# Expert layers: the gate's weights of a batch in 128 zero-padded rows

## The chip, the cores and the metric

The kernel runs on one core of one Trainium2 chip. The metric is the device time of one execution in microseconds (us). A core has a matrix engine (PE, with its weight loads listed apart as PEld), a vector engine (DVE), a scalar engine (ACT), a general engine (POOL), a queue for transfers (SP), and DMA engines. SBUF is its working memory of 128 rows (partitions); PSUM receives the results of PE in banks of 128 rows x 512 values.

## The reference

The whole model is a "macaron" stack: a mixture-of-experts layer (half weight), linear attention, the same expert layer again, six layers of windowed attention with a feed-forward part, a full attention, and the six layers once more. The change touches only the expert layer, which occurs twice:

```python
probs = jax.nn.sigmoid(x_flat @ Wg + bg)
mask = (probs > THRESHOLD).astype(x_flat.dtype)
weights = probs * mask
h = jax.nn.relu(jnp.einsum('td,edh->eth', x_flat, W1) + b1[:, None, :])
expert_out = jnp.einsum('eth,ehd->etd', h, W2) + b2[:, None, :]
combined = jnp.einsum('te,etd->td', weights, expert_out)
```

There are 8 experts, 128 channels, 512 hidden values, and 2048 tokens in 4 batches of 512. Every expert is computed for every token; its output is multiplied by the token's weight for it and summed.

## The kernel before

**Order.** The program has four parts that follow each other: part 0 (the two expert layers and the linear attention between them, class `Front`), part 1 (six layers), part 2 (full attention), part 3 (six layers). Parts 1 and 3 are issued in an order written out by hand, and so is PE's in part 2. In part 0 a scheduler chooses the order of instructions on each engine from a simulated timeline. Storage comes from pools: each tile has a tag, a tag has a fixed number of buffers, and a new tile of a tag waits until the buffer's old tile has been read for the last time. For PSUM the tag mm has four banks, which hold nearly every product in the kernel.

**The expert layer.** `moe` runs 32 steps, expert outside and batch inside. A step does this:

- `hidden` (L274 to L276, then L931 to L937): for each of four blocks of 128 hidden values PE makes hp from three products of 512 columns (values and weights are kept as a high and a low piece; three of the four products of pieces are used). ACT applies bias and relu (L931, tile r), DVE rounds r to the high piece (L935, tile h), and the low piece is the difference (L937), on POOL for the even blocks and on DVE for the odd ones.
- `output` of the step before (L941 to L957): PE spreads the gate's weights of one expert over 128 rows (L945, tile wbp), ACT copies them out of PSUM (L947, wbs), PE accumulates twelve products of 512 columns (L951 to L953, tile o), DVE multiplies o by wbs (L955, tmp), and POOL adds that to acc (L957; DVE for the last expert).
- At the first batch of an expert, `experts` loads its W1 and W2 by DMA (L874, L875) and splits them on ACT and DVE (L811, L812).
- For expert 0 alone, `gates`: logits (tile lg), sigmoid and threshold on DVE and ACT, the weights as high and low piece (wpieces), transposed to rows by PE (L915), copied to wT by ACT (L917), and the part of the bias b2 (L919, L920).

**How the weights lie.** wT is one tile of 128 rows x 512 tokens. Batch b uses its rows 32b to 32b+15: eight experts' high pieces, then eight low pieces. The other rows are never written. The constant `sel` holds, for each expert, a 128 x 128 matrix with ones in rows 32b+e and 32b+8+e for all four b, so that L945, with the 16 rows of one batch on both sides, gives in each of the 128 output rows the weight of expert e for every token. PE's products around it contract 128 rows.

**Where tiles come from.** wT takes the one buffer of tag ge, whose next user is the feed-forward part of part 1 (L630). `begin` makes wT and acc; it runs at the start of each expert layer. Tag E has two buffers of 4096 bytes a row; in part 1 the softmax writes it (L440).

Of the kernel before, what the change touches and what calls it, by code (L numbers as in the profile page):

```python
# [6 lines left out]
F32 = mybir.dt.float32  # L7
FR = mybir.dt.float32r
# [62 lines left out]
def bank(g, tag, shape=(128, 512), name=None):  # L71
    n = math.prod(shape[1:])
    t = g.psum.tile([128, 1024 if tag == "S" else 512], F32, tag=tag, name=name or tag, bufs=BANKS[tag])[0:shape[0], 0:n]
    if len(shape) > 2:
        d = "abcd"[:len(shape) - 1]
        t = t.rearrange("p (%s) -> p %s" % (" ".join(d), " ".join(d)), **dict(zip(d[1:], shape[2:])))
    return t
# [195 lines left out]
def mm3(nc, out, wh, wl, xh, xl):  # L273
    nc.tensor.matmul(out, lhsT=wh, rhs=xh, start=True, stop=False)  # L274
    nc.tensor.matmul(out, lhsT=wh, rhs=xl, start=False, stop=False)  # L275
    nc.tensor.matmul(out, lhsT=wl, rhs=xh, start=False, stop=True)  # L276
# [543 lines left out]
class Front:  # L820
# [71 lines left out]
    def gates(self, b):  # L892

        nc, g = self.nc, self.g
        t = self.xT[b]
        lg = bank(g, "n2", [128, 4, 8], "lg")
        for k in range(4):
            ks = slice(k * 128, (k + 1) * 128)
            mm3(nc, lg[:, k, :], t[:, 0, ks], t[:, 1, ks], self.wg[:, 0, :], self.wg[:, 1, :])
        z = self.tile("z", [128, 4, 8])  # L900
        e = self.tile("e", [128, 4, 8])
        nc.vector.tensor_tensor(z, lg, self.bg.unsqueeze(1).to_broadcast([128, 4, 8]), ALU.add)
        nc.scalar.activation(e, z, AF.Exp, scale=-1.0)
        nc.vector.tensor_scalar(e, e, 1.0, None, ALU.add)
        nc.vector.reciprocal(e, e)
        nc.vector.scalar_tensor_tensor(e, z, 0.0, e, ALU.is_gt, ALU.mult)
        wp = self.tile("wpieces", [128, 4, 2, 8])
        hi = self.tile("whi", [128, 4, 8], FR)
        nc.scalar.copy(hi, e)
        nc.vector.tensor_copy(wp[:, :, 0, :], hi.bitcast(F32))  # L910
        nc.vector.tensor_tensor(wp[:, :, 1, :], e, hi.bitcast(F32), ALU.subtract)
        p = self.bank("wTp")
        rows = slice(32 * b, 32 * b + 16)
        for k in range(4):
            nc.tensor.matmul(p[rows, k * 128:(k + 1) * 128], lhsT=wp[:, k].rearrange("p a c -> p (a c)"), rhs=g.ident,  # L915
                             start=True, stop=True)
        nc.scalar.copy(self.wT[rows], p[rows])  # L917
        p = self.bank("b2p")
        nc.tensor.matmul(p, lhsT=self.b2[rows], rhs=self.wT[rows].bitcast(F32), start=True, stop=True)  # L919
        nc.scalar.copy(self.acc[:, b, :], p)  # L920

    def hidden(self, ex, b):
# [18 lines left out]
    def output(self, ex, b, hs, w2):  # L941
        nc = self.nc
        wb = self.bank("wbp")
        rows = slice(32 * b, 32 * b + 16)
        nc.tensor.matmul(wb, lhsT=self.sel[rows, ex, :], rhs=self.wT[rows], start=True, stop=True)  # L945
        wbs = self.tile("pt", [128, 512], name="wbs")
        nc.scalar.copy(wbs, wb)  # L947
        o = bank(self.g, ("n2", "av")[b % 2], [128, 512], "o")
        for k in range(4):
            h = hs[k]  # L950
            nc.tensor.matmul(o, lhsT=w2[:, 0, k, :], rhs=h[:, 0, :], start=(k == 0), stop=False)  # L951
            nc.tensor.matmul(o, lhsT=w2[:, 1, k, :], rhs=h[:, 0, :], start=False, stop=False)
            nc.tensor.matmul(o, lhsT=w2[:, 0, k, :], rhs=h[:, 1, :], start=False, stop=(k == 3))  # L953
        tmp = self.tile("t2", [128, 512], name="tmp")
        nc.vector.tensor_tensor(tmp, o, wbs, ALU.mult)  # L955
        a = self.acc[:, b, :]
        (nc.vector if ex == 7 else nc.gpsimd).tensor_tensor(a, a, tmp, ALU.add)  # L957
# [7 lines left out]

    def begin(self):
        self.xT = {}
        self.wT = self.tile("ge", [128, 512], FR, "wT")
        self.acc = self.tile("v", [128, 4, 512], name="acc")
        self.experts(0)  # L970

# [387 lines left out]
```

## Time and profile before

| what | value |
|---|---|
| runs | 4488.29, 4487.82, 4475.41 us; median 4487.82 |
| profiled execution | 4486.91 us, of it 4485.1 us from first to last instruction |
| mean granted clock of PE | 0.939 |
| first and second expert layer | about 12 to 270 us and 325 to 580 us |
| linear attention between them | about 270 to 320 us |
| one expert (four steps) in steady running | 27.55 us |
| six layers, full attention, six layers | from about 580, 2250 and 2780 us |

The profile is one execution. "Busy" is the time in which an engine had an instruction under way; PE's instructions overlap, so that the distance between their starts tells more of its pace than their length. A wait names the instruction that ended last before the waiting one started. The chain of waits is followed back from the end of the program, at each step to what released it.

### The profile page before, as it was taken

The numbers are of one execution on the slowest core, as the hardware profiler recorded it, in microseconds if no ns is written. First come the engines' busy times: TensorE is split into PE (matmuls) and PEld (weight loads), VectorE is DVE, ScalarE is ACT, GpSimd is POOL, SyncE is SP. The second block draws the span as 40 slices with busy tenths as digits, with TensorE's granted clock in tenths as the row PEclk, the third lists the DMA queues.
The fourth block names the chain that finished last, engine by engine and source line by source line (L and its number), as shares of the span: only waits on it lengthen the run. The fifth ranks groups of instructions, "written<-read, shape, count | busy, mean of one in ns | idle before, by whom it ended". The sixth has DMA issues, their size and how long they took to land.

```text
span 4485.1 us, 150251 instructions
## 1 busy us (share of the span) xinstructions
PE 3865.4 (86%) x66435; PEld 2663.9 (59%) x66436; DVE 3705.2 (83%) x6415; ACT 2604.5 (58%) x5050; POOL 2493.1 (56%) x2164
## 2 busy tenths in 40 slices
PE   8989978898888888988869998888889889888886
PEld 5666646666666666666533434566666666566665
DVE  6968978888898888888867776888888888888886
ACT  5434455665565565665536666555656656556563
POOL 4625656666666666666501112666666666666663
PEclk9999989999999999999979999999999999999998
DMA  2000033433434334343331222333343343433432
GB/s 61 19 10 15 22 86 74 90 70 81 88 66 91 71 76 88 70 88 73 84 95 49 69 76 52 70 80 82 72 86 73 78 90 61 89 69 77 85 62 49
DMA packets 163852, 312.44 MB, mean 70 GB/s; under 512 B 41304, under 2 KB 125664, under 8 KB 138176
## 3 DMA queue, kind: packets, MB, share of 16 engines
q0 software_dynamic: 31008, 202.40, 22.8%
q1 hardware_dynamic: 132192, 100.44, 7.8%
q8 instruction: 520, 8.52, 0.8%
q14 instruction: 132, 1.08, 0.1%
HBM read 77.49 MB, written 17.69 MB: 21 GB/s over the span
## 4 chain that ended last, share of the span: by engine, by line
DVE 38%; PE 37%; DMA 12%; issue 6%; ACT 4%; POOL 2%; SPq 1%; ACTq 0%; POOLq 0%; DVEq 0%
DMA xs<-x 10%; DVE sm L448 4%; PE vps L401 3%; DVE h L935 3%; DVE E L440 3%; PE S L428 3%; DVE mx L438 3%; DVE xT L269 3%; PE av L471 3%; DVE rtq L308 3%; PE S L1147 2%; DVE pt L455 2%; PE av L1184 2%; PE qkps L274 2%; PE ST L1176 2%
## 5 line engine op out<-in xcount | busy, mean ns | idle before, releaser
L310 POOL TENSOR_TENSOR raw<-raw,rot 128x512 f32<-128x512 f32 x768 | 1006.8, 1362 | 544.2 <-ACT raw L300 540.4
L300 ACT COPY raw<-qkps 128x512 f32<-128x512 f32 x768 | 453.3, 590 | 662.2 <-PE qkps L276 643.7
L401 PE MATMUL vps<-vo,xF 128*32 128x256 f32 x12288 | 751.6, 386 | 40.0 <-issue 29.3
L401 PEld LDWEIGHTS vps<-vo,xF 128*32 128x32 f32 x12288 | 405.9, 111 | 330.3 <-issue 81.6
L452 POOL TENSOR_TENSOR E<-E,smr 128x1024 f32<-128x1024 f32 x192 | 389.6, 2029 | 310.1 <-DVE smr L450 177.0
L407 ACT COPY vx<-vps 128x512 f32<-128x512 f32 x768 | 427.1, 584 | 108.6 <-PE vps L401 106.7
L303 ACT ACTIVATE sq<-qkps 128x512 f32<-128x512 f32 x768 | 473.1, 616 | 0.0
L443 POOL TENSOR_TENSOR E<-E,rq 128x1024 f32<-128x1024 f32 x192 | 388.8, 2025 | 95.6 <-DVE E L440 57.3
L471 PE MATMUL av<-vx,pt 128*32 128x128 f32 x11904 | 381.6, 275 | 58.1 <-DVE x L478 32.8
L274 PE MATMUL qkps<-xT,wqk 128*128 128x512 f32 x768 | 343.4, 447 | 73.3 <-DVE rtq L308 40.6
L471 PEld LDWEIGHTS av<-vx,pt 128*32 128x32 f32 x11904 | 335.7, 110 | 115.8 <-DVE x L478 49.3
L1148 DVE TENSOR_REDUCE nm<-S 128x1 f32<-128x512 f32 x512 | 325.2, 684 | 63.3 <-PE S L1147 62.7
L308 DVE TENSOR_TENSOR rtq<-qkps,rot 128x512 f32<-128x512 f32 x384 | 259.9, 684 | 134.2 <-ACT sq L303 132.6
L383 DVE TENSOR_TENSOR rtk<-rtk,R 128x512 f32<-128x512 f32 x384 | 254.0, 672 | 104.7 <-PE R L380 104.3
L677 PE MATMUL fout<-w,ge 128*128 128x128 f32 (+1 forms) x1152 | 231.9, 379 | 123.3 <-DVE rtk L383 120.4
L1177 ACT ACTIVATE E<-ST 128x512 f32<-128x512 f32 x512 | 273.8, 599 | 109.3 <-PE ST L1176 109.1
L937 POOL TENSOR_TENSOR h<-r,h 128x512 fp32r<-128x512 f32 x128 | 182.3, 1424 | 251.5 <-DVE h L935 237.9
L275 PE MATMUL qkps<-xT,wqk 128*128 128x512 f32 x768 | 310.9, 405 | 5.7 <-issue 2.9
L276 PE MATMUL qkps<-xT,wqk 128*128 128x512 f32 x768 | 309.4, 403 | 5.0 <-issue 5.0
L428 PE MATMUL S<-rtk,rtq 64*32 64x64 f32 (+1 forms) x24576 | 291.4, 229 | 15.5 <-issue 13.3
L428 PEld LDWEIGHTS S<-rtk,rtq 64*32 64x32 f32 x24576 | 284.1, 108 | 31.3 <-issue 18.1
L677 PEld LDWEIGHTS fout<-w,ge 128*128 128x128 f32 (+1 forms) x1152 | 218.4, 289 | 133.7 <-DVE rtk L383 129.4
(257 smaller groups left out, 8803.8 us busy)
## 6 DMA issues: line engine op xcount, KB each, us to landing
rtk<-raw POOLq DMA_DIRECT2D x192, 512.0 KB, 6.7
rtq<-raw POOLq DMA_DIRECT2D x192, 512.0 KB, 6.5
pd<-pc SPq DMA_DIRECT2D x36, 384.0 KB
wqkr<-in_L_ffn_Wqk SPq DMA_DIRECT2D x192, 64.0 KB
rot<-in_c_rot SPq DMA_DIRECT2D x24, 512.0 KB
k<-pd SPq DMA_DIRECT2D x32, 288.0 KB
r<-in_L_ffn_W SPq DMA_DIRECT2D x32, 256.0 KB
wvraw<-in_L_ffn_WvT SPq DMA_DIRECT2D x24, 256.0 KB
```

The costliest lines, as they stand in the source:

```text
L274: nc.tensor.matmul(out, lhsT=wh, rhs=xh, start=True, stop=False)
L300: nc.scalar.copy(raw, ps)
L303: nc.scalar.activation(sq, ps, AF.Square)
L308: nc.vector.tensor_tensor(self.rt[s][:, i, :], ps, rot[:, 0, :], ALU.mult)
L310: nc.gpsimd.tensor_tensor(raw, raw, rot[:, 1, :], ALU.mult)
L401: nc.tensor.matmul(ps[p * 32:(p + 1) * 32, ww, :], lhsT=xF[:, t0:t0 + 32], rhs=g.vo[(self.l, self.hf, p // 2)][:, p % 2, :], start=True, s ...
L407: nc.scalar.copy(self.v[th][:, 2 * t:2 * t + 2, :], ps)
L428: nc.tensor.matmul(self.S[k][p * 32:(p + 1) * 32, ab, w * 64 + 64 - n:w * 64 + 64], lhsT=self.rt[1][rows, p, t0:t0 + 32], rhs=self.rt[0][r ...
L443: nc.gpsimd.tensor_tensor(E4, E4, self.rq[:, :, 8 * k:8 * k + 8].unsqueeze(3).to_broadcast([128, 2, 8, 64]), ALU.mult)
L452: nc.gpsimd.tensor_tensor(E, E, r.unsqueeze(2).to_broadcast([128, 16, 64]), ALU.mult)
L471: g.nc.tensor.matmul(self.av[ww * 32:(ww + 1) * 32, k, :], lhsT=self.pt[w // 8][:, ab, w % 8, role, :], rhs=self.v[src // 8][:, src % 8, a ...
L677: nc.tensor.matmul(self.o[:, t, :], lhsT=h[0:k, t * 128:(t + 1) * 128], rhs=g.F[self.l].w2[0:k, i, :], start=(i == 0 and t == 0), stop=(i ...
```

## The change

wT becomes four arrays of 128 rows x 512 tokens, one for each batch, two to a tile of tag E. Both tiles are filled with zeros on POOL in `begin`. Batch b's 16 rows are written where they were before, at 32b, in its own array. The spreading product takes all 128 rows of `sel` and of the batch's array; the rows of other batches are zero there. The bias product (L919) keeps its 16 rows.

```diff
-        nc.scalar.copy(self.wT[rows], p[rows])
+        nc.scalar.copy(self.wT[b][rows], p[rows])
         p = self.bank("b2p")
-        nc.tensor.matmul(p, lhsT=self.b2[rows], rhs=self.wT[rows].bitcast(F32), start=True, stop=True)
+        nc.tensor.matmul(p, lhsT=self.b2[rows], rhs=self.wT[b][rows].bitcast(F32), start=True, stop=True)
...
         wb = self.bank("wbp")
-        rows = slice(32 * b, 32 * b + 16)
-        nc.tensor.matmul(wb, lhsT=self.sel[rows, ex, :], rhs=self.wT[rows], start=True, stop=True)
+        nc.tensor.matmul(wb, lhsT=self.sel[:, ex, :], rhs=self.wT[b], start=True, stop=True)
...
     def begin(self):
         self.xT = {}
-        self.wT = self.tile("ge", [128, 512], FR, "wT")
+
+        self.wT = []
+        for i in range(2):
+            t = self.tile("E", [128, 2, 512], FR, "wT")
+            self.nc.gpsimd.memset(t.bitcast(F32), 0.0)
+            self.wT += [t[:, 0], t[:, 1]]
         self.acc = self.tile("v", [128, 4, 512], name="acc")
```

In the built program PE's instructions keep their order. POOL has four memsets more: two near its start, two at the end of the first expert layer. The scheduler also reorders some instructions of DVE, ACT and SP in the first 20 us.

## The prediction

> **What bounds the kernel now.** I read the page first, then the stages, the spreading product's own rows, the matrix engine's timeline around it, and last who waits for whom.
>
> ```profile
> span 4485.1 us, 150251 instructions
> PE 3865.4 (86%) x66435; PEld 2663.9 (59%) x66436; DVE 3705.2 (83%) x6415; ACT 2604.5 (58%) x5050; POOL 2493.1 (56%) x2164
> ```
>
> Over the span PE and DVE are both near their limit, and that average does not say which one an edit has to relieve. The change sits in the expert layers alone, so I cut the span into stages (start and end, length, then busy us of each engine with its number of instructions, then the granted clock, DMA share and GB/s).
>
> ```profile
> 0.00:85.00 85.00, 65.29 (x319) 45.83 (x320) 48.97 (x141) 41.96 (x86) 28.07 (x36) 0.96 0.25 74
> 85.00:250.00 165.00, 154.62 (x607) 110.08 (x606) 155.83 (x181) 83.11 (x133) 105.85 (x72) 1.00 0.07 20
> ...
> 330.00:400.00 70.00, 66.60 (x272) 45.79 (x271) 48.10 (x77) 32.43 (x56) 31.33 (x22) 0.93 0.05 16
> 400.00:550.00 150.00, 140.29 (x550) 99.70 (x549) 141.12 (x164) 76.60 (x123) 96.03 (x66) 1.00 0.06 18
> ```
>
> The columns after the length are PE, PEld, DVE, ACT, POOL. In the stretches of experts 1 to 7 (85 to 250 and 400 to 550) DVE is busy 94% of the time; in those of expert 0, with the gates (0 to 85 and 330 to 400), DVE has room (58% and 69%) and PE is the fuller one. The rest of the span, from about 580 us, belongs to other layers.
>
> The product itself, two lines from the groups by shape of the first 620 us:
>
> ```profile
> L945 PE MATMUL wbp<-wT,sel 16*128 16x512 f32 x64 | 31.6, 494 | 1.9 <-ACT r L931 1.9
> L945 PEld LDWEIGHTS wbp<-wT,sel 16*128 16x128 f32 x64 | 11.7, 183 | 26.1 <-ACT r L931 15.3 <-issue 10.4 <-DVE h L935 0.4
> ```
>
> A busy time of 0.49 us says little, since matmuls are pipelined. What counts is the distance between starts (start, duration, instruction):
>
> ```profile
> 188.49 0.39 PE L275 MATMUL hp<-xT,W 128*128 128x512 f32 x1
> 188.72 0.40 PE L276 MATMUL hp<-xT,W 128*128 128x512 f32 x1
> 189.04 0.50 PE L945 MATMUL wbp<-wT,sel 16*128 16x512 f32 x1
> 189.47 0.50 PE L953 MATMUL o<-h,W 128*128 128x512 f32 x1
> 189.81 0.39 PE L951 MATMUL o<-h,W 128*128 128x512 f32 x1
> 190.04 0.39 PE L952 MATMUL o<-h,W 128*128 128x512 f32 x1
> ```
>
> Between products of 128 rows starts lie 0.233 us apart. Into the 16-row product it is 0.32, out of it 0.43, and once more 0.34. The medians over all 64 are 0.327, 0.421 and 0.339, together 1.086 against 3 x 0.233 = 0.699: **0.387 us is lost around each**, with no wait recorded in most of them; 64 x 0.387 = 24.8 us in all, 0.55% of the run.
>
> Now who would profit. Waits from 102 to 250 us (total us, times, longest):
>
> ```profile
> ACT r L931 <- PE hp L276: 42.4, 36, 1.9
> POOL h L937 <- DVE h L935: 38.8, 34, 3.0
> PE o L953 <- POOL h L937: 8.8, 10, 1.1
> DVE h L935 <- ACT r L931: 7.1, 9, 1.3
> ```
>
> DVE waits nine times in 148 us, all at the start of an expert. Elsewhere a cast (L935) starts when DVE's previous instruction ends: in the period from 187 to 211 us the relu result (L931) it reads had been ready for 1.4 to 4.8 us. So DVE, with POOL's subtractions (L937) which delay its casts (0.43 us alone, 1.5 when one runs), sets the 27.55 us of an expert.
>
> **The change, part by part.**
>
> 1. The spreading product contracts 128 rows; in the built program its tile goes from 32 x 128 at row 0, 32, 64 or 96 to 128 x 128, as its neighbours have. Bounds for the three intervals: unchanged (1.086 us) or like the neighbours' (0.699). I take the second: L951 has the same 512 columns and type, and is the nearest row. PE gives back 64 x 0.387 = 24.8 us. The Trainium skill, TensorEngine Tiling, Key Properties, states that a change of tiling mode drains the engine; the intervals here, 0.387 us over three starts, agree, and with every drain on the path the sum would be 24.8 us. The same skill's TensorE: Matmul & The Clock Gate, Why this matters for your kernels, says that a K=32 product takes the time of a K=128 one, which speaks against any gain from more rows; by it alone the sum would be zero, and this trace cannot separate rows from mode.
>
> 2. How much lies on the path. Steady experts: nothing. After the L945 at 202.62 PE stands idle 1.06 and 0.70 us for POOL's h (at 204.83 and 207.19); what is won ahead of these goes into that wait. From 207.19 PE runs the stretch that DVE does wait for (four o products, then hp's, then L931), and L945 is not in it. The one at 211.31 waits for L931 itself. So these are worth 0. In expert 0 and just after it the chain of waits runs through nine of them, at 49.9, 75.3, 80.6, 350.6, 359.2, 376.1, 382.3, 388.7 and 394.9 us: at most 9 x 0.387 = 3.5 us. From DVE's timeline: no gap from 74.4 to 98 us, so 75.3 and 80.6 give nothing; none from 359 to 364, so 359.2 gives nothing; after 394.9 PE waits again for POOL at 397.35, which ended at 397.29. Left: 0.39 at 49.9, 0.39 at 350.6, 0.78 for 376.1 and 382.3 (DVE idles 0.82 us at 386.72) and 0.30 for 388.7 (DVE idles 0.30 at 392.64): **1.9 us**. If DVE's cover were gone the full 24.8 would show.
>
> 3. Four memsets of 128x1024 on POOL. No such row; between zt (128x256, 357 ns) and vx (128x1344, 1223 ns) the slope is 0.796 ns per element, so 0.97 us each. Bounds: 0.36 and 1.22. The first two come ahead of the identity's second half (ended at 3.24) and of the load of spread; it then ends near 4.6, the first transposes that need it start at 12.09. POOL's start-up work ended at 6.3 and its first L937 was at 18.29: hidden. The third waits for the product at 251.32 and stands ahead of two L937:
>
> ```profile
> 254.11 1.40 POOL L937 TENSOR_TENSOR h<-r,h 128x512 fp32r<-128x512 f32 x1 [1.43 <-DVE h L935]
> 258.73 1.28 POOL L937 TENSOR_TENSOR h<-r,h 128x512 fp32r<-128x512 f32 x1 [3.21 <-DVE h L935]
> ```
>
> It fits from 255.5 into the 3.21 us idle. The fourth waits for the last product (261.57), then has POOL to itself until about 330; the copies into wT (L917) come later. I take 0 for all; without cover the third would cost 0.97, and if a memset stops DVE as L937 does, 1 us twice.
>
> 4. Start-up order. The scheduler reorders some DVE, ACT and SP instructions of the first 20 us. ACT now copies wg and half of W (0.18 and 0.61 us) ahead of block 0's normalisation (L108 at 11.71). That copy waits for its load, which had landed by 12.65, when SP reused its semaphore: L108 at worst 12.65 + 0.61 + 0.2 = 13.46, +1.75 us. On the other side the load of spread (0.5 MB) is issued about 2 us later and leaves the DMA engines to x: x, sel and spread (2.1 MB) took some 8.9 us, so up to -2.2 us. These nearly cancel; I take 0. On SP two 512 KB loads for linear attention move past three small ones (L162, L163, one L179); of these only L179's is read soon, by L182 on ACT, which now stands behind the first L931.
>
> 5. Storage. wT moves from tag ge to both buffers of E. E's next writer is L440 at 620 us, 59 us after the last product; ge then is free early. PE's order is unchanged throughout; from the first L1 block on, POOL, DVE, ACT and SP keep theirs too, with one exception in waits: 12 vps groups (L401) of the last block get other banks. Taken as 0.
>
> Sum: 4486.91 (profiled execution, 1.8 around its span) - 1.9 = 4485.0; the median of the runs is 0.9 above that execution, so **4485.9 us**.
>
> **The rivals.**
>
> PE-bound: if the steady experts do follow PE (PE never waits for 20 us there, which speaks for it; DVE's slack of 1.4 us and more speaks against), nearly all of 24.8 us appears: 4463.
>
> Nothing happens: the lost time hangs on the product's wait for a bank or on its weights, not on its tile. For: 15.3 us of idle weight load before it is put down to L931. Against: the same 0.387 where no wait is recorded. Time: 4487.8.
>
> Slower: the 12 vps groups of the last block wait for DVE's L308 where they waited for ACT's L407, or the reverse. If in each swap DVE is later by one L308 (684 ns), 12 x 0.68 = 8.2 us: 4496. It decides once DVE is more than one instruction behind PE there; for it, DVE is 83% busy; against, five of the twelve change from ACT to DVE, five from DVE to ACT, and two stay with ACT.
>
> **How the numbers follow.** Forecast 0.74, PE-bound 0.10, nothing 0.08, slower 0.08. About 0.3% is what a measurement of this kernel can tell from no change (the three runs lie 12.9 us apart). Faster than 4474.4 are PE-bound and a twentieth from the forecast's own scatter: 0.15. Slower than 4501.3 only with the vps waits and scatter together: 0.07. The rest is 0.78. Range: from the lowest run less the gain and part of the rival (4468) to the slower rival (4496). The forecast's own: 4474 to 4491.
>
> **What would show it.** L945 as 128*128 with 0.233 us on both sides; PE's idle time before L953 up by about 1 us per expert; the period of an expert still 27.5 us; memsets of about 1 us without a waiter. Wrong if the period falls below 27 us (then PE bounded), or if the stretch from 2780 us on is longer by more than 5 us.

## The result, and the profile after

The changed kernel takes 4477.01 us (median of 22 runs, 4462.51 to 4488.7); the kernel before, run beside it, 4487.56 us (22 runs). The ratio is 0.9976, 95% interval 0.9965 to 0.9987: about 10.5 us or 0.24% less. The interval does not reach 1.0000, so the gain is real, but it lies within the 0.3% that the prediction called no change. Forecast were 4485.9 us.

First the page after: span, busy time of each engine with its share and instructions, and the two lines on the chain that ended last; behind it the second of these two lines of the kernel before.

```profile
span 4479.9 us, 150253 instructions
PE 3861.3 (86%) x66435; PEld 2677.1 (60%) x66436; DVE 3722.1 (83%) x6415; ACT 2605.4 (58%) x5050; POOL 2496.9 (56%) x2168
...
DVE 39%; PE 36%; DMA 10%; issue 6%; ACT 4%; POOL 3%; SPq 0%; ACTq 0%; POOLq 0%; DVEq 0%
DMA xs<-x 8%; DVE sm L448 3%; DVE h L935 3%; PE vps L401 3%; DVE E L440 3%; DVE mx L438 3%; PE S L428 3%; DVE xT L269 3%; PE av L471 3%; DVE rtq L308 3%; PE S L1151 2%; PE av L1188 2%; PE fout L677 2%; PE qkps L274 2%; DVE pt L455 2%
```

```profile
DMA xs<-x 10%; DVE sm L448 4%; PE vps L401 3%; DVE h L935 3%; DVE E L440 3%; PE S L428 3%; DVE mx L438 3%; DVE xT L269 3%; PE av L471 3%; DVE rtq L308 3%; PE S L1147 2%; DVE pt L455 2%; PE av L1184 2%; PE qkps L274 2%; PE ST L1176 2%
```

The engines' busy shares have hardly moved, and the four instructions more on POOL are the memsets. One entry of the chain is clearly smaller: the load of xs had 10% before and has 8% now. It belongs to the twelve layers of parts 1 and 3, which the change does not touch.

Lines shift a little: the product is L944 now, the products behind it L950 to L952, the memset L971. The product's group by shape in the first 620 us, and PE's timeline around one of them (start, duration, instruction):

```profile
L944 PE MATMUL wbp<-wT,sel 128*128 128x512 f32 x64 | 26.3, 411 | 1.9 <-ACT r L931 1.9
```

```profile
192.70 0.39 PE L276 MATMUL hp<-xT,W 128*128 128x512 f32 x1
192.93 0.39 PE L944 MATMUL wbp<-wT,sel 128*128 128x512 f32 x1
193.16 0.39 PE L952 MATMUL o<-h,W 128*128 128x512 f32 x1
193.39 0.39 PE L950 MATMUL o<-h,W 128*128 128x512 f32 x1
```

The three intervals are 0.23 us each; their medians over all 64 are 0.236, 0.231 and 0.232, together 0.699 where they were 1.086. Now the steady experts, two stretches moved by 4 us so that they hold nearly the same work as before, and the waits from 106 to 254 us (total us, times, longest).

```profile
89.00:254.00 165.00, 149.37 (x605) 110.44 (x604) 155.88 (x181) 82.97 (x133) 105.95 (x72) 1.00 0.07 20
404.00:554.00 150.00, 134.61 (x542) 98.74 (x541) 140.94 (x165) 75.13 (x121) 95.22 (x65) 1.00 0.08 22
```

```profile
PEld o L952 <- POOL h L937: 21.6, 20, 1.9
...
PE o L952 <- POOL h L937: 12.8, 15, 1.5
...
DVE h L935 <- ACT r L931: 7.0, 9, 1.3
```

PE is busy 5.3 us less in the first stretch (154.62 before), DVE exactly as long (155.83 before). The wait of PE for POOL's h has grown from 8.8 to 12.8 us and DVE's for ACT is 7.0 instead of 7.1. The period of an expert, the median distance from one expert's first spreading product to the next one's (from expert 2 on), is 27.58 and 27.59 us in the two layers against 27.57 and 27.53 before. What PE wins, PE waits.

So the gain is elsewhere. From each trace I took three marks: the end of the first expert layer and the end of part 0 (both at the last addition into x, L964 before), and the first write of E (L440), with which the twelve layers' attention begins. "Half clock" is the time at a granted clock of 0.5; the record of the clock begins 17 to 27 us into each trace.

| execution | first expert layer ends | part 0 ends | half clock, first 100 us | half clock, about 290 to 440 us | first E to the end of the span |
|---|---|---|---|---|---|
| before | 271.0 | 569.7 | 6.8 | 23.9 | 3865.0 |
| before_again | 271.2 | 569.9 | 10.2 | 23.9 | 3868.3 |
| after | 275.8 | 580.4 | 20.5 | 34.1 | 3848.9 |
| after_again | 274.8 | 579.4 | 20.5 | 34.1 | 3846.2 |

Two effects oppose each other: **part 0 is 10 us longer, and what follows it is 16 to 22 us shorter.** Part 0 holds all the work that was changed; its loss falls where PE's clock does. From expert 0's first spreading product to expert 1's it takes 51.2 and 48.2 us in the two layers, where before it took 47.0 and 43.9. The same windows of the kernel before and of the changed one (PE, PEld, DVE, ACT, POOL busy, then granted clock, DMA share, GB/s):

```profile
40.00:60.00 20.00, 19.16 (x73) 12.45 (x74) 9.29 (x21) 9.98 (x18) 5.66 (x4) 0.83 0.05 14
60.00:80.00 20.00, 17.85 (x127) 13.69 (x126) 10.16 (x20) 11.42 (x22) 7.14 (x5) 1.00 0.22 66
...
340.00:360.00 20.00, 19.20 (x92) 13.08 (x91) 12.02 (x27) 9.18 (x18) 8.66 (x6) 1.00 0.04 15
```

```profile
40.00:60.00 20.00, 19.34 (x70) 13.16 (x70) 7.99 (x16) 8.66 (x15) 5.27 (x4) 0.72 0.05 14
60.00:80.00 20.00, 18.15 (x116) 14.04 (x115) 7.84 (x16) 10.49 (x21) 4.54 (x4) 0.83 0.22 66
...
340.00:360.00 20.00, 19.13 (x70) 13.31 (x69) 7.70 (x20) 6.70 (x14) 4.84 (x4) 0.70 0.00 0
```

PE is as busy in both, but gets less done (116 products instead of 127 from 60 to 80 us at a clock of 0.83 instead of 1.00; 70 instead of 92 from 340 to 360 us at 0.70 instead of 1.00, where the changed kernel is also some 5 us behind). These are the stretches of expert 0 and its gates. The steady experts run at 1.00 in both.

The shorter part shows in one wait. L609 is the first of DVE's reads of xs, a load of x shifted by a row; before and after:

```profile
L609 DVE BATCH_NORM_STATS2 bst<-xs x192: 172/173/228, 683.7 to 4461.5; 128x6 f32<-128x64 f32 x192
...
  DMA xs<-x: 98.7, 38
```

```profile
L609 DVE BATCH_NORM_STATS2 bst<-xs x192: 172/173/229, 691.1 to 4456.6; 128x6 f32<-128x64 f32 x192
...
  DMA xs<-x: 75.0, 28
```

DVE stands 98.7 us in 38 waits for this load before, and 75.0 us in 28 after. That is 23.7 us less, and the part from the first E on is 16.1 us shorter. The memsets themselves last as forecast, and nothing waits for them:

```profile
L971 POOL MEMSET wT<- x4: 962/974/987, 2.0 to 266.9; 128x1024 f32 x4
```

### The profile page after: what moved, and what is told of

Same layout as the page of the kernel before. It is cut to its first block, busy times and chain, and to the rows that moved or that the text cites. A ratio compares the mean times of both kernels' runs of the same rounds, so it can differ in the third digit from the quotient of the medians.

```text
span 4479.9 us, 150253 instructions
## 1 busy us (share of the span) xinstructions
PE 3861.3 (86%) x66435; PEld 2677.1 (60%) x66436; DVE 3722.1 (83%) x6415; ACT 2605.4 (58%) x5050; POOL 2496.9 (56%) x2168
## 4 chain that ended last, share of the span: by engine, by line
DVE 39%; PE 36%; DMA 10%; issue 6%; ACT 4%; POOL 3%; SPq 0%; ACTq 0%; POOLq 0%; DVEq 0%
DMA xs<-x 8%; DVE sm L448 3%; DVE h L935 3%; PE vps L401 3%; DVE E L440 3%; DVE mx L438 3%; PE S L428 3%; DVE xT L269 3%; PE av L471 3%; DVE rtq L308 3%; PE S L1151 2%; PE av L1188 2%; PE fout L677 2%; PE qkps L274 2%; DVE pt L455 2%
## 5 line engine op out<-in xcount | busy, mean ns | idle before, releaser
L1181 ACT ACTIVATE E<-ST 128x512 f32<-128x512 f32 x512 | 273.9, 599 | 108.2 <-PE ST L1180 108.0
```

## The experiments

Twelve experiments ran, in four groups: nine new kernels and three repeats. Each group shared its own runs of the kernel before, on one chip.

**Both kernels once more, and the product undone alone.** rows16 is the changed kernel with its storage and memsets and the old product:

```diff
-        nc.tensor.matmul(wb, lhsT=self.sel[:, ex, :], rhs=self.wT[b], start=True, stop=True)
+        rows = slice(32 * b, 32 * b + 16)
+        nc.tensor.matmul(wb, lhsT=self.sel[rows, ex, :], rhs=self.wT[b][rows], start=True, stop=True)
```

> The kernel before, unchanged, for a second profile. Theory A (the gain of 10.5 us is the product's): the stage from 2780 us to the end takes about 1705 us, as in the first profile, and so does the front (part 0, to the first write of E at 620 us). Theory B (each stage scatters by several us from one execution to the next, so that one pair of profiles cannot place the gain): front and last six layers differ from the first profile by 5 us or more each, with nothing changed.

> The changed kernel, for a second profile and for times on the same chip as the next one. Both theories: 0.9965 to 0.9987 of before. Theory A: front about 11 us longer than before's and the last six layers about 14 us shorter, as in the first pair of profiles. Theory B: another division.

> The changed kernel with the spreading product put back to 16 rows on both sides (same output); four arrays, tag E, memsets and every engine's order as in the changed kernel. Theory P (the product's tile makes the gain): 4487 us, 0.999 to 1.001 of before, and 0.387 us lost around each product again. Theory L (storage addresses, start-up order or memsets make it): 4477 us, 0.9965 to 0.9987.

before_again took 4489.84 us in its one run, after_again 4477.78 (0.9977, 0.9963 to 0.9992), rows16 4472.19 (0.9968, 0.9955 to 0.9982). The gain stays without the 128-row product, so it is not the product's; theory P falls and L stands, for the moment. rows16 ends part 0 at 570.3 us, without the 10 us of loss.

Of the theories on the two repeats, A holds for part 0, 9.5 to 10.7 us longer in both profiles. For the place of the gain it does not hold: from the first write of E in part 3 to the end the kernel before takes 1685.7 and 1681.6 us and the changed one 1668.0 and 1678.5, while from the first to the last write of E in part 1 it is 1613.4 and 1622.7 us against 1615.4 and 1604.3. So the gain lay in part 3 in the first pair and mostly in part 1 in the second; one program's stages scatter by some 10 us from execution to execution.

**Where part 0 loses, and which move of storage gains.** ex0_rows16 takes 16 rows for expert 0 alone, ex0_rows128 128 rows for expert 0 alone:

```diff
+        rows = slice(32 * b, 32 * b + 16) if ex == 0 else slice(0, 128)
```

shift2k and e_first start from the kernel before and move its buffers, by a pad ahead of wT or by E's two buffers there:

```diff
+        pad = self.tile("pad", [128, 512])
+        self.nc.gpsimd.memset(pad, 0.0)
         self.wT = self.tile("ge", [128, 512], FR, "wT")
```

```diff
+        for i in range(2):
+            t = self.tile("E", [128, 2, 512], FR)
+            self.nc.gpsimd.memset(t.bitcast(F32), 0.0)
         self.wT = self.tile("ge", [128, 512], FR, "wT")
```

> The changed kernel, with expert 0's eight products put back to 16 rows and the other 56 left at 128; storage, memsets and every engine's order are the changed kernel's. The front end is the time from the span's start to the last addition into x of the second MoE (569.7 and 569.9 us in the two profiles of before, 570.3 with all products at 16 rows, 580.4 and 579.4 in the two of the changed kernel). Theory C, the ten us of the front are lost at the gates of expert 0, where the 128-row products go with twice as much time at half clock: the front ends at about 570 us, half clock in the first 100 us is about 10 us and not 20.5, and the time is about 4472 us (0.9968 of before). Rival C2, the products of experts 1 to 7 lose them: the front ends at about 579 us and the time stays at 4477. Rival C3, it is chance in where the clock's windows fall: the front ends at either, whatever the rows.

> The counterpart: expert 0's eight products at 128 rows, the other 56 at 16. Theory C: the front ends at about 579 us with some 20 us at half clock in the first 100 us, and the time is about 4478 us. Rival C2: the front ends at about 570 us, time 4472. Rival C3: either.

> The kernel before, with a buffer of 2048 bytes that nothing reads placed ahead of ge (and cleared twice on POOL): rows and ge's use as before, and raw, rtk, rtq, E, pt and all between them 2048 bytes higher, as in the changed kernel; 49 of the 3947 PSUM tiles follow another tile in their bank than before, most of them vps. Theory S, the move by 2048 bytes is what shortens the stall on xs: the stalls ahead of L609 add up to about 70 us in the twelve layers and not 92 to 95, the front ends at 570, and the time is about 4472. Rival B, the 12 vps groups of the last block that take other banks shorten it: no shorter stall in the first six layers, which have none of them, and about 4485 to 4488 unless this kernel's own bank changes do the same. Rival N, the twelve layers scatter from one build to the next: anything from 4470 to 4490.

> The kernel before, with the two buffers of E placed ahead of ge and cleared as the changed kernel clears them, and wT left in ge in its 32-row slices with the 16-row product: every PSUM tile lies in the bank that it has in the changed kernel, E's buffers at the changed kernel's addresses, while ge, raw, rtk, rtq and pt lie 8192 bytes higher than before and not 2048. Theory S in its narrow form (2048 bytes count): about 4485 to 4488, stalls ahead of L609 92 to 95 us. Theory S in its wide form (any move, or E's place) and rival B (the banks of the 12 vps groups): about 4472, stalls ahead of L609 about 70 us; under B only the last six layers are shorter, about 1621 us where before had 1636 and 1634, and the first six keep 1613 to 1623. Rival N: anything from 4470 to 4490.

| kernel | median us | ratio (95%) | first expert layer ends | part 0 ends | half clock, first 100 / 290 to 440 us | first E to end |
|---|---|---|---|---|---|---|
| ex0_rows16 | 4473.89 | 0.9970 (0.9958 to 0.9982) | 272.7 | 575.7 | 10.2 / 37.5 | 3842.1 |
| ex0_rows128 | 4477.63 | 0.9975 (0.9962 to 0.9988) | 276.7 | 580.6 | 20.5 / 34.1 | 3843.0 |
| shift2k | 4486.03 | 0.9998 (0.9986 to 1.0010) | 275.8 | 575.0 | 17.1 / 23.9 | 3853.8 |
| e_first | 4474.35 | 0.9962 (0.9949 to 0.9976) | 274.1 | 576.0 | 17.1 / 34.1 | 3862.2 |

The narrow theory of a 2048-byte move falls with shift2k, whose waits for xs still add up to 96.3 us. e_first, with 16 rows and other addresses, has the gain in its timed runs (its profiled one, 4490.2 us, is the slowest of six and shows no short layers). Of C and its rivals none comes out clean. C2 falls, since expert 0's products alone at 128 rows give 580.6. But with 16 rows there, part 0 ends at 575.7, between the two forecasts, and the time follows the half clock of each layer more than the rows.

So I looked at what sets the clock. The half-speed stretches last whole multiples of 3.41 us, but for the last one of each trace. I divided each trace into windows of 3.41 us and worked out what share of each one PE spent streaming: the columns of its products at 213 ns for 512. Over all fourteen profiles, a full-speed window with a share under 0.32 was followed by half speed 991 times in 1034, one from 0.32 to 0.40 112 times in 232, one from 0.40 to 0.60 105 times in 957, and one from 0.60 to 1.00 13 times in 3400; where products on small tiles overlap the sum exceeds 1, and none of those windows was followed by it. In the first 620 us alone it is 104 of 110, 11 of 51, 5 of 410 and none of 1535. The 213 ns rest on the 2.4 GHz that the Trainium skill, TensorE: Matmul & The Clock Gate, Part 1: The HAM clock gate, gives; by the trace's 0.233 us between starts the shares are a tenth larger. The same section names a free-running window of 3413 ns, which these stretches bear out, and a fall to half rate after an idle window; here the fall comes after windows in which PE streamed up to a third of the time, so the trace corrects "idle". This is a count of what goes together; from 0.32 to 0.40 the share does not tell which way a window goes.

At expert 0's gates PE waits often, and its windows lie near that range. Take the kernel before and ex0_rows128, the timeline from the same place (start, duration, instruction):

```profile
39.29 0.25 PE L275 MATMUL lg<-wg,xT 128*128 128x8 f32 x1
39.41 0.25 PE L276 MATMUL lg<-wg,xT 128*128 128x8 f32 x1
39.52 0.25 PE L274 MATMUL lg<-wg,xT 128*128 128x8 f32 x1
```

```profile
39.57 0.35 PE L275 MATMUL lg<-wg,xT 128*128 128x8 f32 x1
39.78 0.35 PE L276 MATMUL lg<-wg,xT 128*128 128x8 f32 x1
39.99 0.35 PE L274 MATMUL lg<-wg,xT 128*128 128x8 f32 x1
```

Up to 38.5 us the two lists of starts agree within 0.03 us, but for the products from 33.5 to 35.3 us: with 128 rows those behind the spreading product start up to 0.4 us earlier, and by 35.5 us they are back at their old times. So the window from 35.1 to 38.5 us holds a share of 0.357 (before: 0.399), the next one is granted half speed, and the gate's small products lie 0.21 us apart and not 0.11. In the two profiles of the changed kernel this window has 0.346, and half speed after it; in before_again, rows16 and ex0_rows16 0.349, 0.391 and 0.400, and full speed. In the second expert layer the window at about 344 us has 0.350 to 0.370 in the three with 128 rows, half speed after it, and 0.388 in before, before_again and rows16, full speed after it.

That the lower share is what costs the clock is argued and not shown. before_again kept full speed behind 0.349, and rows16_nm, of the next group, behind 0.365 in the second layer. Nor does it take 128 rows: with 16, e_first, shift2k and rows16_again (of the last group) fell to half speed at about 40 us as well, behind windows of 0.268 to 0.295, which begin 1.0 to 1.5 us later than the one before it at 35.1 us.

**Two questions by themselves: the storage without the memsets, and a filled window.** rows16_nm drops the memsets from rows16, which are not needed with 16 rows. fill3 issues expert 0's products three times:

```diff
-            self.nc.gpsimd.memset(t.bitcast(F32), 0.0)
```

```diff
+        for _ in range(1 if ex else 3):
+            nc.tensor.matmul(wb, lhsT=self.sel[:, ex, :], rhs=self.wT[b], start=True, stop=True)
```

> The 16-row product in the changed kernel's storage, without the four memsets (no row beyond the sixteen is read): every buffer lies at the changed kernel's address, and every one of the 3947 PSUM tiles in the bank that it has in the kernel before. Theory D, where E, ge and the buffers behind them lie in SBUF is what makes the twelve layers shorter: about 4472 us (0.997), the stalls ahead of L609 add up to 63 to 76 us, and the mean time from the issue of xs to L609 in the first six layers is 12.2 to 12.6 us (12.24 to 12.62 in the five profiles with this storage, 12.77 to 13.13 in the four without). Rival B, the banks of the 12 vps groups make them shorter: about 4487 us (1.000), the last six layers take 1634 to 1636 us as before and not 1614 to 1630. If the stalls are short and the time is not, neither is the cause alone.

> The changed kernel, with each of expert 0's eight products issued three times (the same values written again, 16 products of 512 columns more, 0.233 us each, 3.7 us of PE in all); some vps groups take other banks than in the changed kernel. Theory T, the clock of each 3.41 us window follows from how much of the window before PE streamed (512 columns at 2.4 columns per ns is 213 ns): windows with a share under 0.32 are followed by half clock, those above 0.40 by full clock, and the 128-row product took the windows at the gates of expert 0 from 0.349 to 0.401 down to 0.346 to 0.357 in the first MoE and from 0.388 to 0.350 to 0.369 in the second. Two products more are 0.125 of a window: the window stays full, half clock in the first 100 us falls from 20.5 to about 10 us, the front ends at 570 to 574 us and not at 580, and the time is some 5 us under the changed kernel's, if the banks cost nothing. Rival W, the lost time comes from something else at the gates and the clock only goes along: 16 more products make it longer by up to 3.7 us, and the front ends at 580 to 584 us.

rows16_nm: 4488.57 us, 1.0007 (0.9995 to 1.0019). **The gain is gone, at the changed kernel's addresses.** Theory D falls. From the first E on it takes 3861.2 us, and its wait for xs is back (rows16, then rows16_nm):

```profile
L609 DVE BATCH_NORM_STATS2 bst<-xs x192: 171/174/229, 680.7 to 4434.8; 128x6 f32<-128x64 f32 x192
...
  DMA xs<-x: 69.3, 30
```

```profile
L609 DVE BATCH_NORM_STATS2 bst<-xs x192: 171/173/229, 683.3 to 4460.8; 128x6 f32<-128x64 f32 x192
...
  DMA xs<-x: 95.8, 43
```

fill3: 4476.64 us, 0.9979 (0.9967 to 0.9991), no better than the changed kernel, and part 0 ends at 584.8 us, where theory T had 570 to 574 and rival W 580 to 584. The filled window did reach a share of 0.613, but the one after it had 0.268 and fell in its place, so that the first 100 us keep 20.5 us at half clock. In the second layer half clock went from 34.1 to 27.3 us and the products added cost about as much. As a remedy it failed, and T's time was missed by more than 10 us; that half speed comes behind a window with a low share was seen here again.

**The banks alone.** rows16 and rows16_nm differ in the memsets, in the order that the scheduler gives the first 20 us, and in the banks of 12 vps groups. nm_own is rows16_nm with each mm bank written out in a list, its own; nm_banks has the changed kernel's list:

```diff
+    if tag == "mm":
+        k = getattr(g, "mm", 0)
+        g.mm = k + 1
+        tag, bufs = "mm" + MM[k], 1
```

> rows16_nm (16-row product, the changed kernel's storage, no memsets) with the bank of each of its 3453 mm tiles given by a written list, the list being rows16_nm's own choice. This moves some instructions in the first MoE, so it is the base for nm_banks alone. Theories B and O both: about 4488 us, as rows16_nm (1.0007), give or take what the reordered start does.

> nm_own with the changed kernel's list of banks: the order of every engine's instructions, every address in SBUF and every other bank succession are nm_own's, and only the 12 vps groups of the last block, at five places, follow another tile in their bank. Theory B (these 12 groups bring the gain): 12 to 15 us under nm_own (0.997 of it), the last six layers near 1621 us where nm_own has near 1633. Theory O (the gain comes with another order at the start, where three of SP's transfers and some 20 of DVE's instructions change places when the memsets are there, and the banks only go along): the same as nm_own within 4 us.

> The changed kernel with the 16-row product again, beside the two on one chip: 0.9955 to 0.9982 of before as the first time (4472 us there) if its gain is a property of the program; near 1.000 if the first was chance of that chip. Under B it is as fast as nm_banks, under O faster than both.

| kernel | median us | ratio (95%) | first expert layer ends | part 0 ends | half clock, first 100 / 290 to 440 us | first E to end |
|---|---|---|---|---|---|---|
| nm_own | 4470.42 | 0.9974 (0.9961 to 0.9987) | 277.1 | 560.3 | 17.1 / 3.4 | 3870.7 |
| nm_banks | 4470.29 | 0.9967 (0.9952 to 0.9983) | 277.8 | 561.1 | 20.5 / 3.4 | 3863.1 |
| rows16_again | 4468.78 | 0.9977 (0.9965 to 0.9989) | 273.9 | 575.8 | 17.1 / 34.1 | 3838.9 |

nm_own and nm_banks have medians 0.1 us apart and means 3.1 us apart (standard error 3.5, from the scatter of 12 and 7 runs), where rival B asked for 12 to 15. Nor do the banks go with the short layers elsewhere: fill3, in which 55 tiles follow another one than in the changed kernel, takes 3841.5 us from the first E on. That nm_own is fast at all was forecast by neither. Its gain is another one: the written list moves instructions around expert 0 in both expert layers and in the linear attention between them, and a few far behind, near the start of part 3 (the expectation named the first layer only). The second gates keep nearly full clock (3.4 us at half instead of 23.9), and part 0 ends at 560.3 us; from the first E on the profiled execution is as slow as before, with the old stall (its read of xs is at L644):

```profile
L644 DVE BATCH_NORM_STATS2 bst<-xs x192: 171/173/231, 676.3 to 4457.5; 128x6 f32<-128x64 f32 x192
...
  DMA xs<-x: 109.3, 41
```

That profile is the slowest of nm_own's twelve runs, 12.6 us above their median. If the median run writes E first at 610.5 us too, some 3858 us are left behind it, an estimate: most of its gain is then part 0's. Nor are all other profiles typical: nm_banks' is the slowest of seven, rows16's the fastest of eleven.

rows16_again repeats rows16's gain, and shows how much the clock's windows do by chance. It is the same program as rows16, yet part 0 ends at 575.8 us and not 570.3. Of rows16, then of rows16_again:

```profile
60.00:80.00 20.00, 17.82 (x127) 13.61 (x126) 10.15 (x20) 11.43 (x22) 7.16 (x5) 1.00 0.22 66
340.00:360.00 20.00, 19.20 (x93) 13.16 (x91) 11.80 (x27) 8.72 (x18) 8.66 (x6) 1.00 0.05 14
```

```profile
60.00:80.00 20.00, 18.34 (x111) 14.12 (x111) 6.59 (x15) 10.63 (x20) 3.53 (x4) 0.74 0.18 53
340.00:360.00 20.00, 19.19 (x82) 13.04 (x81) 11.17 (x26) 8.75 (x17) 7.08 (x6) 0.83 0.00 1
```

At 0.74 PE issued 111 products from 60 to 80 us where it issued 127 at 1.00. This is rival C3, and it holds beside C: with 16 rows at expert 0 part 0 ended anywhere from 569.7 to 576.0 us in the eight profiles without the written list, and in all four with 128 rows there at 579.4 us or later.

## Why the prediction came out, and where it did not

No change beyond 0.3% was forecast and measured, and the time lies in the range; but of the sum two terms taken as 0 or nearly 0 were large in the profiles, with opposite signs: part 0 lost some 10 us, and the layers behind it won 16 to 22. The 10.5 us gained are what these two left, and not the 1.9 us that were forecast by way of expert 0. That the time lies in the range owes more to luck than to the reasoning; what the reasoning had right is that the product's own gain does not reach the end.

Step 1 (0.387 us around each product): right. 1.086 - 0.699 = 0.387 us, as taken; by the neighbours' bound and not the unchanged one. The reading by which more rows change nothing is out for this stream of products; whether the rows or the change of tile cost the 0.387 us, no run separates.

Step 2, steady experts worth nothing: right, with the period 0.01 and 0.06 us longer and PE's wait for POOL up by 4.0 us in 148, some 0.75 us per expert where 1 was named. **Step 2, the 1.9 us in expert 0: failed, by the profiles in sign.** Single gains of 0.3 to 0.4 us do show there, and are lost again. I followed the chain of waits at the clock that before was granted, as if the edit could not alter it. The clock's record shows in its place 54.6 us at half clock in the first 100 us and from 290 to 440 us, where the kernel before had 30.7 and 34.1, and part 0 came out 9.5 to 10.7 us longer in the profiles of the changed kernel. That finishing 0.3 us earlier lowered the share of a window and so the clock fits the windows at 35 us, but a window of 0.349 that kept full speed speaks against a plain edge, so that this way stays argued. In medians this loss is at most a few microseconds: the kernels with 128 rows at expert 0 and one product each have 0.9976, 0.9977 and 0.9975, those with 16 rows and the same start 0.9968, 0.9977 and 0.9970, and the intervals overlap. The chance in rows16_again makes the rows' own share uncertain.

Step 3 (memsets of 0.97 us, hidden): right for their duration, 0.974 us, and for waiters, of which there are none; whether they are without effect is step 4's question.

**Step 4 (start-up order, -2.2 to +1.75, taken as 0) failed in its bounds, or step 3's 0 for the memsets did.** For the first 20 us themselves the bounds held: L108 starts at 12.12 us instead of 11.71. But I priced nothing else. rows16 has the gain (0.9968 and 0.9977) and rows16_nm, at the same addresses, has not (1.0007); the banks do not bring it. What is left between them is the four memsets and the order at the start, where two of SP's loads move ahead of three small ones and some DVE, ACT and POOL instructions change places. e_first, with four such memsets, all at the start, and the changed kernel's order of DVE and SP there, at other addresses, has the gain too (0.9962). shift2k, beside it on one chip, clears a buffer of half the size twice (128x512, 0.54 us each) and has DVE and ACT in another order at the start, but SP's transfers in the order of the kernel before, and has no gain (0.9998). It differs in addresses and banks as well; still, a memset or another order of DVE and ACT is not enough by itself. The gain is worth 13 to 18 us (1.0007 less 0.9977 or 0.9968, of 4488), and it does not appear at the start but in the layers, as a shorter wait for xs: 3838 to 3849 us from the first E on in the seven profiles that have the memsets in the changed storage, 3854 to 3871 in the six that lack them or have another pad; e_first's one slow profile is the exception with 3862.2. DVE's waits for xs divide in the same way, 69.3 to 85.0 us against 95.8 to 109.3, with 91.2 in e_first's profile. How an order 600 us earlier comes to shorten that wait is **not settled**. The four long memsets and SP's new order go together in every kernel that ran, so they could not be told apart: one without the other was not run. Rival N, chance from build to build, is not excluded by a mechanism either; against it, six kernels with this start have the gain, and before, shift2k and rows16_nm without it have not.

Step 5 (storage 0, banks 0): right in both. rows16_nm gives 1.0007 for the addresses, and nm_banks against nm_own -0.1 us for the 12 groups. So the slower rival's swaps cost nothing that the runs can tell.

Of the other rivals, the PE-bound one fails by the period; that nothing happens at the tile fails by the intervals. Of the two signs of error that I named, the period stayed above 27 us, and the stretch from 2780 us on was not longer but shorter.

No version beats the changed kernel by more than the intervals: rows16, nm_own and nm_banks lie at 0.9967 to 0.9977. nm_own's short part 0 and rows16's short layers seem to come from different causes and were not combined.

## What to carry to other kernels

Padding a 16-row product to 128 rows bought exactly the interval the neighbours promised, 0.387 us each. In the steady experts none of it reached the end, because another engine set the period. Before trusting a gain or a loss of a few tenths of a per cent, undo the edit's core and keep its side effects (storage, memsets, order): here that one kernel kept the whole gain. And look at the granted clock by stretch ahead of pricing microseconds on a chain: a chain followed at one clock says little where the clock itself may change, as it did here in the stretches where PE was short of work.

## What the hardware showed beyond that

PE's clock was granted in steps of 3.41 us, and went with the work streamed in the step before: half speed after 96% of the full-speed windows with a share under 0.32, after 0.4% of those from 0.60 to 1.00, and after about half of those from 0.32 to 0.40. At 35 us windows of 0.346 and 0.357 lost full speed and one of 0.349 kept it, so that the share as counted here is not the whole rule. Two executions of one program ended part 0 5.5 us apart with different windows. And DVE's total wait for the 48 loads of xs, 69.3 us in one profile and 109.3 in another, went in 13 of 14 profiles with the memsets and the order of the program's first 20 us, hundreds of microseconds earlier; the way from the one to the other stays open.
